# A mixture-of-experts tail on one Trainium2 core: pair table on ScalarE, another pair numbering, a shorter lead, more of the weighted sum on TensorE

## The chip, the cores and the metric

The kernel runs on one core of one Trainium2 chip. The metric is the device time of one execution in microseconds (us). A core has five engines with instruction queues of their own: TensorE (PE, with its weight loads shown apart as PEld), VectorE (DVE), ScalarE (ACT), GpSimd (POOL) and SyncE (SP), which here issues the plain DMA transfers; POOL issues the indirect ones (gathers and scatters by an index table).

## The reference

A decoder of two layers works on 8 sequences of 128 tokens of 256 numbers, all float32. Each layer has attention, cross-attention and a feed-forward part, with a layer normalisation after each. The change touches only the last part, a mixture of 64 experts of which each token uses 8:

```python
logits = x @ gate_w.T                       # 1024 tokens, 64 experts
probs = softmax(logits); w, idx = top_k(probs, 8)
combine = (one_hot(idx, 64) * w[..., None]).sum(axis=1)
for e in range(64):
    h = silu(x @ w13[e][:128].T) * (x @ w13[e][128:].T)
    acc += combine[:, e:e+1] * (h @ w2[e].T)
x = layernorm(x + acc)
```

## The kernel before

Up to about 676 us the kernel computes everything ahead of the experts; this part is the same in both versions, but for one small POOL operation. After that come four stages.

**The pair table (L845 to L879).** There are 1024 x 8 = 8192 pairs of a token and a chosen expert. They are sorted by expert into 64 blocks (NG) of 128 rows. For each pair its place in the sorted order is known (`blk_f`, `row_f`), and the inverse is wanted: which pair stands at each place. It is found with 0/1 matrices. For each of the 8 sequences b, DVE makes `is_blk` (L852, 8 x 64 per token) and `is_row` (L862, 8 x 128). ACT multiplies `is_blk` by the token's row number plus one into `no[:, 0]` (L857), and POOL multiplies it by the turn number b*8+k+1 into `no[:, 1]` (L858, with the row `turn_no`). Eight matmuls per sequence (`pair_in`, L868) add these up in PSUM, all sequences into one result, with the row in its one half and the turn in its other. Five DVE operations (L872 to L879) turn this into `pairs`, the row of the DRAM array `pair_rows` to which a pair's result is written, and `tok_i`, the token to gather. The pair number is (b*8 + k)*128 + s for token s of sequence b.

**The visits (`run_visits`).** A block may hold rows of several experts, so the unit of work is a visit of one expert to one block. Here 104 visits (FEW, the arm "few") are executed. Visit and block have the helpers:

- `gather(g)`, L923: POOL gathers the 128 token rows of block g by an indirect DMA into a ring of 6 buffers `xg`.
- `turn(g)`, L933 and L934: PE transposes the block, and DVE copies it from PSUM into its place in the long array `cols`.
- `fetch(v)`, L943: SP fetches the expert's weights of visit v, 384 KB, into the ring `wring` of 10 buffers.
- `hidden(v)`, L955: eight matmuls; then Silu on ACT (L963) and the product on DVE (L965). `begins` gives the column at which the visit begins, as a register.
- `down(v)`, L972: four matmuls, and ACT copies the result back into `cols` (L975) over the input.
- `turn_back(g)`, L982 to L985: PE transposes the finished block, DVE copies it, and POOL scatters its rows to `pair_rows`.
- `weight(b)` (L888 to L895) and `spread(b)` (L903) on DVE: the eight combine weights of each token of sequence b, and for each of the first ON_PE = 4 of them a 128 x 128 diagonal matrix `diag`.

The order on PE and POOL is written by hand as one loop over steps. The other engines' order is set by a scheduler. The loop's body, for steps from -8:

```python
if 0 <= step < count:            hidden(step)
if 0 <= step + LEAD < NG:        turn(step + LEAD)        # LEAD = 4
if 0 <= step - 2 < count:        down(step - 2)
if 0 <= step + 8 < count:        fetch(step + 8)
if 0 <= step + 8 < NG:           gather(step + 8)
if 0 <= step - 3 - spare < NG:   turn_back(step - 3 - spare)
if 0 <= step < 12 * B and step % 12 == 11: weight(...); spread(...)
```

`spare` is 104 - 64 = 40: block g can be written over by visits up to g + 40, so its scatter comes 43 steps after.

**The tail (L1022 to L1039).** For each sequence SP loads its 8 x 128 pair rows, 1 MB, into a tile `z` (L1027) of a pool with four buffers. PE adds up the first four of the eight weighted terms by matmuls with the diagonals (`moe_sum`, L1030, each float32 matmul being two instructions), DVE adds the other four to the residual (L1034), then the two are added (`moe_r`, L1036) and normalised (`layernorm`: L177, L179 and L182 on DVE, L171 and L172 on POOL between them). SP writes the result `y` out (L1039).

Of the kernel before, what the change touches and what calls it, by code (L numbers as in the profile page):

```python
# [9 lines left out]
F32 = mybir.dt.float32  # L10
I32 = mybir.dt.int32
BF16 = mybir.dt.bfloat16
AF = mybir.ActivationFunctionType
ALU = mybir.AluOpType
AX = mybir.AxisListType

P = 128
B = 8
# [14 lines left out]
TOP = 8  # L33
NG = B * S * TOP // P
# [20 lines left out]
def decoder_kernel(ctx: ExitStack, tc: tile.TileContext, i, out):  # L55
    nc = tc.nc
# [21 lines left out]
    def ps_mm(name):  # L78
        return ps_of["mm"].tile([P, 512], F32, tag="mm", name=name)
# [366 lines left out]
    with tc.tile_pool(name="l0f", bufs=1) as fp:  # L446
# [51 lines left out]
        with tc.tile_pool(name="l0fh", bufs=1) as hp:  # L498
            for h in range(HALVES):
# [8 lines left out]
                for bb in range(4):  # L508
                    b = 4 * h + bb
# [17 lines left out]
    zd = dp.tile([B * TOP * S, D], F32, name="pair_rows")  # L527
    rp = ctx.enter_context(tc.tile_pool(name="route", bufs=1))
# [6 lines left out]
    iota = rp.tile([P, P], F32, name="iota")  # L535
# [2 lines left out]
    nc.gpsimd.iota(starts, pattern=[[P, P]], base=0, channel_multiplier=0, allow_small_or_imprecise_dtypes=True)  # L538
    row_no = rp.tile([P, 1], F32, name="row_no")
    nc.gpsimd.iota(row_no, pattern=[[1, 1]], base=1, channel_multiplier=1, allow_small_or_imprecise_dtypes=True)  # L540
    turn_no = rp.tile([P, B * TOP], BF16, name="turn_no")
    nc.gpsimd.tensor_scalar(turn_no, iota[:, : B * TOP], 1.0, None, ALU.add)
    comb = rp.tile([P, B, NE], F32, name="combine")
    seen = rp.tile([P, B + 1, NE], F32, name="seen")
    nc.gpsimd.memset(seen[:, 0, :], 0.0)
# [21 lines left out]
    with l1w, tc.tile_pool(name="l1a", bufs=2) as ap, tc.tile_pool(name="l1v", bufs=L1_HEADS + 2) as vp:  # L567
        scale = 1.0 / math.sqrt(P)
# [216 lines left out]
    loop = ExitStack()  # L785
# [61 lines left out]
    with tc.tile_pool(name="onehot", bufs=3) as op:  # L847
        pn = ps_mm("pair_in")[:, : 2 * NG].rearrange("p (a g) -> p a g", a=2)
        for b in range(B):
            at = slice(b * TOP, (b + 1) * TOP)  # L850
            is_blk = op.tile([P, TOP, NG], BF16, tag="is_blk", name=f"is_blk_{b}")
            nc.vector.tensor_tensor(  # L852
                is_blk, iota[:, :NG].unsqueeze(1).to_broadcast([P, TOP, NG]),
                blk_f[:, at].unsqueeze(2).to_broadcast([P, TOP, NG]), ALU.is_equal,
            )
            no = op.tile([P, 2, TOP, NG], BF16, tag="no", name=f"no_{b}")
            nc.scalar.activation(no[:, 0], is_blk, AF.Copy, scale=row_no)  # L857
            nc.gpsimd.tensor_tensor(  # L858
                no[:, 1], is_blk, turn_no[:, at].unsqueeze(2).to_broadcast([P, TOP, NG]), ALU.mult
            )  # L860
            is_row = op.tile([P, TOP, P], BF16, tag="is_row", name=f"is_row_{b}")
            nc.vector.tensor_tensor(  # L862
                is_row, iota.unsqueeze(1).to_broadcast([P, TOP, P]),
                row_f[:, at].unsqueeze(2).to_broadcast([P, TOP, P]), ALU.is_equal,
            )
            for k in range(TOP):
                n = b * TOP + k
                nc.tensor.matmul(  # L868
                    pn, is_row[:, k, :], no[:, :, k, :], start=(n == 0), stop=(n == B * TOP - 1)
                )  # L870
    s_of = rp.tile([P, NG], F32, name="s_of")
    nc.vector.tensor_scalar(s_of, pn[:, 0], -1.0 - P, None, ALU.add)  # L872
    pairs = rp.tile([P, NG], I32, name="pairs")
    nc.vector.scalar_tensor_tensor(pairs, pn[:, 1], float(P), s_of, ALU.mult, ALU.add)
    tok_b = rp.tile([P, NG], I32, name="tok_b")
    nc.vector.tensor_scalar(tok_b, pairs, 10, 7, ALU.arith_shift_right, ALU.logical_shift_left)
    tok_i = rp.tile([P, NG], I32, name="tok_i")
    nc.vector.tensor_single_scalar(tok_i, pairs, P - 1, op=ALU.bitwise_and)
    nc.vector.tensor_tensor(tok_i, tok_i, tok_b, ALU.bitwise_or)  # L879


    cw = rp.tile([P, B, TOP], F32, name="pair_weight")
    wring = loop.enter_context(tc.tile_pool(name="wring", bufs=10, side="right"))
    mp = loop.enter_context(tc.tile_pool(name="moe", bufs=3, side="right"))

    def weight(b):
# [8 lines left out]
        nc.vector.reduce_sum(cw[:, b, :], eq, axis=AX.X)  # L895


    ON_PE = 4
    diag = dgp.tile([P, B, ON_PE, P], F32, name="diag")

    def spread(b):
        for k in range(ON_PE):
            nc.vector.tensor_scalar(diag[:, b, k, :], ident, cw[:, b, k : k + 1], None, ALU.mult)  # L903

    LEAD = 4

    def run_visits(arm, count):

# [12 lines left out]
        def gather(g):  # L921
            x = mp.tile([P, D], F32, tag="xg", bufs=6, name=f"xg_{arm}_{g}")
            nc.gpsimd.indirect_dma_start(  # L923
                out=x, out_offset=None, in_=xd,
                in_offset=bass.IndirectOffsetOnAxis(ap=tok_i[:, g : g + 1], axis=0),
                bounds_check=B * S - 1, oob_is_err=False,
            )
            xg[g] = x

        def turn(g):  # L930
            pt = ps_tr(f"moe_xT_{arm}_{g}").rearrange("p (k t) -> p k t", k=4)[:, :2]
            for k in range(2):
                nc.tensor.transpose(pt[:, k, :], xg[g][:, k * P : (k + 1) * P], ident)  # L933
            nc.vector.tensor_copy(cols[:, :, (g + 1) * P : (g + 2) * P], pt)  # L934
# [14 lines left out]
        def hidden(v):  # L949
            o = begins(v, nc.tensor.engine, fed)  # L950
            ps = ps_mm(f"moe_gu_{arm}_{v}")[:, :D].rearrange("p (a t) -> p a t", a=2)
            for a in range(2):
                for k in range(2):
                    at = k * D + a * P
                    mm = nc.tensor.matmul(  # L955
                        ps[:, a, :], ws[v][:, at : at + P], cols[:, k, bass.ds(o + P, P)],
                        start=(k == 0), stop=(k == 1),
                    )

                    tc.declare_no_dep(mm.ins, group=f"left_{arm}", reason="columns of earlier visits")  # L960
            fed.append(mm.ins)
            s = mp.tile([P, P], F32, tag="s", name=f"moe_s_{arm}_{v}")
            nc.scalar.activation(s, ps[:, 0, :], AF.Silu)  # L963
            hid = mp.tile([P, P], F32, tag="hid", bufs=4, name=f"moe_h_{arm}_{v}")
            nc.vector.tensor_tensor(hid, ps[:, 1, :], s, ALU.mult)  # L965
            hs[v] = hid

        def down(v):
            ps = ps_o(f"moe_o_{arm}_{v}")[:, :D].rearrange("p (c t) -> p c t", c=2)
            for c in range(2):  # L970
                at = 2 * D + c * P
                nc.tensor.matmul(ps[:, c, :], ws[v][:, at : at + P], hs[v], start=True, stop=True)  # L972
            o = begins(v, nc.scalar.engine, left)

            cp = nc.scalar.copy(cols[:, :, bass.ds(o, P)], ps)  # L975
            left.append(cp.ins)
            tc.add_to_no_dep_group(f"left_{arm}", cp.ins)
# [17 lines left out]
        with tc.manual_schedule(engines={nc.tensor.engine, nc.gpsimd.engine}):  # L995
            for step in range(-8, count + 4):
                if 0 <= step < count:
                    hidden(step)
                if 0 <= step + LEAD < NG:
                    turn(step + LEAD)  # L1000
                if 0 <= step - 2 < count:
                    down(step - 2)
                if 0 <= step + 8 < count:
                    fetch(step + 8)
                if 0 <= step + 8 < NG:
                    gather(step + 8)
                if 0 <= step - 3 - spare < NG:
                    turn_back(step - 3 - spare)
                if 0 <= step < 12 * B and step % 12 == 11:
                    weight(step // 12)  # L1010
                    spread(step // 12)
# [5 lines left out]
    with tc.If(few == NE) as enough:  # L1017
        run_visits("few", FEW)
    with enough.Else():
        run_visits("all", NV)  # L1020

    loop.close()  # L1022
    tp = ctx.enter_context(tc.tile_pool(name="tail", bufs=4, side="right"))
    zv = zd.rearrange("(b k s) d -> b s k d", b=B, k=TOP)
    for b in range(B):
        z = tp.tile([P, TOP, D], F32, tag="z", name=f"z_{b}")
        nc.sync.dma_start(out=z, in_=zv[b])  # L1027
        ps = ps_mm(f"moe_sum_{b}")[:, :D]
        for k in range(ON_PE):
            nc.tensor.matmul(ps, diag[:, b, k, :], z[:, k, :], start=(k == 0), stop=(k == ON_PE - 1))  # L1030

        acc = x5[b // 2][:, b % 2, :]
        for k in range(ON_PE, TOP):
            nc.vector.scalar_tensor_tensor(acc, z[:, k, :], cw[:, b, k : k + 1], acc, ALU.mult, ALU.add)  # L1034
# [67 lines left out]
```

## Time and profile before

| | us |
|---|---|
| median of 3 runs (lowest, highest) | 964.62 (963.94, 969.0) |
| the profiled execution | 968.18 |
| its span, from first to last instruction | 966.5 |
| pair table: first is_blk to the end of tok_i | 676.55 to 699.79 |
| first gather issued | 700.84 |
| first hidden starts | 708.83 |
| last scatter issued | 917.29 |
| first z issued, first moe_sum | 921.58, 927.60 |
| last y computed (end) | 963.23 |

Times within the profile count from the start of its span. The profile lists for each engine which work was busy when, what ended an idle time (the releaser), and which share of full speed the TensorE clock was granted (0.909 over the span). A group of instructions is named by line, engine and the tensors out<-in. A matmul's end is modelled. The DMA figures are the busy share of the core's 16 DMA engines and the rate.

### The profile page before, as it was taken

How to read it: one execution, taken by the hardware profiler on the slowest of the kernel's cores; microseconds unless marked ns; L12 is line 12 of the kernel's file. 1: busy time of each engine (PE TensorE's matmuls, PEld its weight loads, DVE VectorE, ACT ScalarE, POOL GpSimd, SP SyncE). 2: the span in 40 equal slices, each digit the busy share in tenths (PEclk: the TensorE clock that was granted, in tenths of full speed). 3: DMA queues.
4: the chain of work that ended last, by engine and by line, in shares of the span. 5: the costliest groups of instructions: out<-in, count | busy, mean ns of one | idle time of the engine just before them, and what ended most of it. 6: DMA issues, size and time to landing. Idle time of an engine off the chain costs nothing.

```text
span 966.5 us, 14470 instructions
## 1 busy us (share of the span) xinstructions
PE 825.1 (85%) x4650; PEld 557.1 (58%) x4650; DVE 484.6 (50%) x1312; ACT 280.3 (29%) x968; POOL 249.1 (26%) x333
## 2 busy tenths in 40 slices
PE   7999976699999999999989699994369986999743
PEld 3555533356655557755547455552259986988632
DVE  2899655421344442344441377765867342433346
ACT  2677411022133331133330033321213331333200
POOL 0000144201400000000000623111776665554611
PEclk9999977589999999999998799986569998999968
DMA  7800000410000000000000100000449986888475
GB/s 234 308 1 2 1 1 0 123 59 1 0 1 1 0 1 1 0 1 0 1 1 1 43 2 13 13 12 12 163 129 305 328 299 195 265 290 294 132 230 169
DMA packets 46259, 87.66 MB, mean 91 GB/s; under 512 B 6112, under 2 KB 23872, under 8 KB 46176
## 3 DMA queue, kind: packets, MB, share of 16 engines
q1 hardware_dynamic: 40032, 69.85, 22.5%
q0 software_dynamic: 6144, 16.79, 5.1%
q8 instruction: 42, 0.69, 0.3%
q14 instruction: 41, 0.34, 0.1%
HBM read 76.13 MB, written 10.49 MB: 90 GB/s over the span
## 4 chain that ended last, share of the span: by engine, by line
PE 64%; DVE 15%; POOL 7%; issue 5%; DMA 4%; ACT 2%; another core or an unknown queue 1%; SPq 1%; POOLq 0%; ACTq 0%; DVEq 0%
PE moe_gu_few L955 8%; PE l_y L609 6%; PE l_v L577 6%; PE l_q L577 6%; PE l_k L577 6%; PE moe_o_few L972 4%; PE l_c L600 3%; PE l_s L592 3%; PE down L514 3%; PE y_s L662 3%; PE up L504 2%; DVE maxima L668 2%; DVE l_e L220 2%; ACT l_e L213 2%; PE moe_xT_few L933 2%
## 5 line engine op out<-in xcount | busy, mean ns | idle before, releaser
L213 ACT ACTIVATE l_e<-l_s,nm_l 128x128 f32<-128x128 f32 x256 | 90.2, 368 | 109.2 <-DVE nm_l L210 108.9
L955 PE MATMUL moe_gu_few<-cols,w_few 128*128 (+1 forms) x832 | 116.6, 285 | 1.5 <-issue 0.6
L955 PEld LDWEIGHTS moe_gu_few<-cols,w_few 128*128 128x128 f32 x832 | 106.1, 200 | 5.6 <-issue 5.2
L985 POOL DMA_INDIRECT pair_rows<-moe_os_few,pairs x64 | 63.4, 991 | 54.7 <-DVE moe_os_few L984 35.9
L923 POOL DMA_INDIRECT xg_few<-x_rows,tok_i x64 | 66.3, 1036 | 36.2 <-issue 14.0
L171 POOL TENSOR_SCALAR rs_l1a<-mv_l1a 128x1 f32<-128x1 f32 x8 | 1.8, 221 | 269.2 <-DVE mv_l1a L179 269.2
L972 PE MATMUL moe_o_few<-moe_h_few,w_few 128*128 128x128 f32 x416 | 65.9, 282 | 0.0
L691 ACT ACTIVATE y_e<-y_sT 128x512 f32<-128x512 f32 x64 | 33.0, 604 | 94.5 <-PE y_sT L684 94.5
L577 PE MATMUL l_q<-xT_l1a,w_qkv 128*128 128x512 f32 x128 | 60.2, 593 | 0.0
L577 PE MATMUL l_v<-xT_l1a,w_qkv 128*128 128x512 f32 x128 | 60.1, 592 | 0.0
L577 PE MATMUL l_k<-xT_l1a,w_qkv 128*128 128x512 f32 x128 | 60.1, 592 | 0.0
L609 PE MATMUL l_y<-w_o,l_vs 128*128 128x256 f32 x256 | 57.3, 387 | 0.0
L972 PEld LDWEIGHTS moe_o_few<-moe_h_few,w_few 128*128 128x128 f32 x416 | 57.0, 199 | 0.1
L220 DVE TENSOR_SCALAR l_e<-l_e,inv_l 128x128 f32<-128x128 f32 x256 | 55.7, 282 | 1.4
L963 ACT ACTIVATE moe_s_few<-moe_gu_few 128x128 f32<-128x128 f32 x104 | 28.9, 279 | 92.4 <-PE moe_gu_few L955 39.5
L609 PEld LDWEIGHTS l_y<-w_o,l_vs 128*128 128x128 f32 x256 | 50.0, 196 | 8.5 <-issue 1.5
L934 DVE COPY cols<-moe_xT_few 128x256 f32<-128x256 f32 x64 | 26.9, 421 | 52.6 <-PE moe_gu_few L955 17.9
L213 ACT ACTIVATION_READ_ACCUMULATOR l_e<-l_s,nm_l 128x1 f32 x256 | 52.9, 206 | 0.0
L601 DVE TENSOR_TENSOR l_vs<-l_c,l_vs 128x512 f32<-128x512 f32 x32 | 22.1, 692 | 60.5 <-PE l_c L600 60.5
L975 ACT COPY cols<-moe_o_few 128x256 f32 (+1 forms) x104 | 38.8, 373 | 44.4 <-PE moe_o_few L972 11.6
L965 DVE TENSOR_TENSOR moe_h_few<-moe_gu_few,moe_s_few 128x128 f32<-128x128 f32 x104 | 29.7, 287 | 41.5 <-ACT moe_s_few L963 25.8
L210 DVE TENSOR_REDUCE nm_l<-l_s 128x4 f32<-128x512 f32 x64 | 43.3, 686 | 10.6 <-PE l_s L592 8.6
(258 smaller groups left out, 1430.6 us busy)
## 6 DMA issues: line engine op xcount, KB each, us to landing
w_few<-in_experts SPq DMA_DIRECT2D x104, 384.0 KB
z<-pair_rows SPq DMA_DIRECT2D x8, 1024.0 KB
w_qkv<-in_w_qkv SPq DMA_DIRECT2D x8, 768.0 KB
w_o<-in_w_o SPq DMA_DIRECT2D x1, 2048.0 KB
xT<-in_xT SPq DMA_DIRECT2D x2, 512.0 KB
x<-in_x SPq DMA_DIRECT2D x4, 256.0 KB
cx<-in_ctx SPq DMA_DIRECT2D x1, 1024.0 KB
q_up<-in_up_qT SPq DMA_DIRECT2D x4, 256.0 KB
```

Of the source, the lines that this page charges most:

```text
L210: nc.vector.tensor_reduce(nm, s, AX.X, ALU.max, negate=True)
L213: nc.scalar.activation(e[:, a, :], s[:, a, :], AF.Exp, bias=nm[:, a : a + 1], scale=1.0, accum_out=sums[:, a : a + 1],)
L220: nc.vector.tensor_scalar(e[:, a, :], e[:, a, :], inv[:, a : a + 1], None, ALU.mult)
L577: nc.tensor.matmul(ps, w_qkv[:, k, c, n, :], xT[h][:, k, :], start=(k == 0), stop=(k == 1))
L609: nc.tensor.matmul(py[:, :D], scaled[h, m][:, bb * S : (bb + 1) * S], w_o[:, m, :], start=(m == 0), stop=(m == L1_HEADS - 1),)
L691: nc.scalar.activation(e, tiles[j], AF.Exp)
L923: nc.gpsimd.indirect_dma_start(out=x, out_offset=None, in_=xd, in_offset=bass.IndirectOffsetOnAxis(ap=tok_i[:, g : g + 1], axis=0), bounds ...
L955: mm = nc.tensor.matmul(ps[:, a, :], ws[v][:, at : at + P], cols[:, k, bass.ds(o + P, P)], start=(k == 0), stop=(k == 1),)
L965: nc.vector.tensor_tensor(hid, ps[:, 1, :], s, ALU.mult)
L972: nc.tensor.matmul(ps[:, c, :], ws[v][:, at : at + P], hs[v], start=True, stop=True)
L975: cp = nc.scalar.copy(cols[:, :, bass.ds(o, P)], ps)
L985: inst = nc.gpsimd.indirect_dma_start(out=zd, out_offset=bass.IndirectOffsetOnAxis(ap=pairs[:, g : g + 1], axis=0), in_=o, in_offset=None, ...
```

## The change

Six edits, all in the last part of the kernel:

1. `no[:, 1]` is made by ACT, in eight activations of 128 x 64 with the turn number as an immediate scale, instead of one POOL operation of 128 x 512. `no[:, 0]` is multiplied by eight times the row number (`row_8`, which takes the place of `turn_no`).
2. The pair number is now token*8 + k, with the token b*128 + s. Six DVE operations make `pairs` and `tok_i` instead of five.
3. `LEAD` is 2 instead of 4, and the gather is issued 6 steps ahead instead of 8. The ring `xg` still has 6 buffers.
4. `ON_PE` is 6 instead of 4: 48 diagonals instead of 32, six terms on PE and two on DVE per sequence.
5. `wring` has 9 buffers instead of 10.
6. The tail's pool has 8 buffers instead of 4. With the new numbering the 8 pair rows of one token lie together, so that z is read in pieces of 8 KB per partition instead of eight of 1 KB.

The order on PE and POOL stays as the loop gives it. SP's order in the tail is z0, z1, z2, z3, out0, z4, out1, z5, out2, out3, z6, out4, z7 and the rest of out; before it was z0 to z3, out0, out1, z4, out2, z5, out3, z6, out4, z7.

```diff
-    turn_no = rp.tile([P, B * TOP], BF16, name="turn_no")
-    nc.gpsimd.tensor_scalar(turn_no, iota[:, : B * TOP], 1.0, None, ALU.add)
+    row_8 = rp.tile([P, 1], F32, name="row_8")
+    nc.gpsimd.tensor_scalar(row_8, row_no, 8.0, None, ALU.mult)
...
-            nc.scalar.activation(no[:, 0], is_blk, AF.Copy, scale=row_no)
-            nc.gpsimd.tensor_tensor(
-                no[:, 1], is_blk, turn_no[:, at].unsqueeze(2).to_broadcast([P, TOP, NG]), ALU.mult
-            )
+            nc.scalar.activation(no[:, 0], is_blk, AF.Copy, scale=row_8)
+            for k in range(TOP):
+                nc.scalar.activation(no[:, 1, k], is_blk[:, k], AF.Copy, scale=float(b * TOP + k + 1))
...
-    s_of = rp.tile([P, NG], F32, name="s_of")
-    nc.vector.tensor_scalar(s_of, pn[:, 0], -1.0 - P, None, ALU.add)
+    n_of = rp.tile([P, NG], I32, name="n_of")
+    nc.vector.tensor_scalar(n_of, pn[:, 1], -1.0, None, ALU.add)
+    seq = rp.tile([P, NG], I32, name="seq")
+    nc.vector.tensor_scalar(seq, n_of, 3, 10, ALU.arith_shift_right, ALU.logical_shift_left)
+    nc.vector.tensor_single_scalar(n_of, n_of, TOP - 1, op=ALU.bitwise_and)
+    nc.vector.tensor_tensor(n_of, n_of, seq, ALU.bitwise_or)
     pairs = rp.tile([P, NG], I32, name="pairs")
-    nc.vector.scalar_tensor_tensor(pairs, pn[:, 1], float(P), s_of, ALU.mult, ALU.add)
-    tok_b = rp.tile([P, NG], I32, name="tok_b")
-    nc.vector.tensor_scalar(tok_b, pairs, 10, 7, ALU.arith_shift_right, ALU.logical_shift_left)
+    nc.vector.scalar_tensor_tensor(pairs, pn[:, 0], -8.0, n_of, ALU.add, ALU.add)
     tok_i = rp.tile([P, NG], I32, name="tok_i")
-    nc.vector.tensor_single_scalar(tok_i, pairs, P - 1, op=ALU.bitwise_and)
-    nc.vector.tensor_tensor(tok_i, tok_i, tok_b, ALU.bitwise_or)
+    nc.vector.tensor_single_scalar(tok_i, pairs, 3, op=ALU.arith_shift_right)
...
-    wring = loop.enter_context(tc.tile_pool(name="wring", bufs=10, side="right"))
+    wring = loop.enter_context(tc.tile_pool(name="wring", bufs=9, side="right"))
...
-    ON_PE = 4
+    ON_PE = 6
...
-    LEAD = 4
+    LEAD = 2
...
-                if 0 <= step + 8 < NG:
-                    gather(step + 8)
+                if 0 <= step + 6 < NG:
+                    gather(step + 6)
...
-    tp = ctx.enter_context(tc.tile_pool(name="tail", bufs=4, side="right"))
-    zv = zd.rearrange("(b k s) d -> b s k d", b=B, k=TOP)
+    tp = ctx.enter_context(tc.tile_pool(name="tail", bufs=B, side="right"))
+    zv = zd.rearrange("(b s k) d -> b s k d", b=B, k=TOP)
```

## The prediction

> **What bounds the kernel now.** The profiled execution took 968.18 us: a span of 966.5 and 1.68 around it. The median of the runs shown is 964.62, so I work on the profiled time and subtract 3.6 at the end. About 0.5% (4.8 us) is what a measurement of this kernel can tell from no change. Nothing before the pair table at 676 us is touched but one small POOL operation, so I read first the busy time by stage (window, length, then busy us and instructions of PE, PEld, DVE, ACT, POOL, then granted clock, DMA share, GB/s):
>
> ```profile
> 680.00:700.00 20.00, 8.07 (x64) 6.65 (x63) 16.75 (x18) 4.33 (x6) 14.84 (x8) 0.50 0.49 185
> 700.00:720.00 20.00, 10.75 (x66) 9.46 (x67) 11.54 (x30) 2.84 (x7) 14.08 (x13) 0.67 0.30 82
> 720.00:760.00 40.00, 40.00 (x334) 39.78 (x333) 27.58 (x85) 14.47 (x46) 24.99 (x24) 0.93 0.93 310
> 760.00:800.00 40.00, 35.98 (x310) 34.50 (x309) 15.02 (x47) 13.14 (x43) 25.08 (x25) 1.00 0.90 306
> 800.00:840.00 40.00, 32.83 (x237) 30.78 (x238) 15.06 (x44) 9.97 (x32) 22.78 (x24) 0.87 0.73 218
> ...
> 940.00:966.00 26.00, 9.32 (x32) 6.58 (x32) 16.22 (x40) 0.00 (x0) 4.82 (x12) 0.84 0.59 186
> ```
>
> The limits differ by stage: DVE and POOL in the table (680 to 700), PE in the visits after 720, with the DMA close behind; in the tail no engine is full. The waits name them (engine, line, releaser: us in total, times, longest):
>
> ```profile
> PE moe_sum L1030 <- DMA z<-pair_rows: 23.1, 5, 13.1
> ...
> PE pair_in L868 <- POOL no L858: 14.3, 7, 6.6
> ...
> PE moe_xT_few L933 <- DVE cols L934: 10.8, 4, 3.2
> ```
>
> The timeline of the table's last two sequences shows the period (start, duration, engine, operation):
>
> ```profile
> 678.42 0.67 DVE L852 TENSOR_TENSOR is_blk<-iota,blk_f 128x512 bf16<-128x512 f32 x1
> ...
> 693.14 1.89 POOL L858 TENSOR_TENSOR no<-is_blk,turn_no 128x512 bf16<-128x512 bf16 x1 [0.69 <-DVE is_blk L852]
> 694.05 1.52 DVE L852 TENSOR_TENSOR is_blk<-iota,blk_f 128x512 bf16<-128x512 f32 x1
> ...
> 695.67 0.72 ACT L857 ACTIVATE no<-is_blk,row_no 128x512 bf16<-128x512 bf16 x1 [1.86 <-DVE is_blk L852]
> 695.72 1.89 POOL L858 TENSOR_TENSOR no<-is_blk,turn_no 128x512 bf16<-128x512 bf16 x1 [0.69 <-DVE is_blk L852]
> ```
>
> POOL's product starts every 2.58 us (693.14, 695.72), and is_blk takes 1.52 beside it, 0.67 when alone. And the tail's last sequences:
>
> ```profile
> 953.70 0.41 DVE L182 TENSOR_SCALAR y<-moe_r,mv_l1f,rs_l1f 128x256 f32<-128x256 f32 x1 [0.98 <-POOL rs_l1f L172]
> 954.03 2.04 DVE L1034 SCALAR_TENSOR_TENSOR x<-z,pair_weight,x 128x256 f32<-128x256 f32 x4
> ...
> 955.90 1.97 PE L1030 MATMUL moe_sum<-z,diag 128*128 128x256 f32 x8 [2.08 <-DMA z<-pair_rows]
> 956.17 0.42 DVE L1036 TENSOR_TENSOR moe_r<-moe_sum,x 128x256 f32<-128x256 f32 x1
> ```
>
> DVE goes round in 4.57 us (y at 953.70, the next at 958.27), 2.04 of it for four weighted additions; PE sums a sequence in 1.97 and waits for z.
>
> [...]two Silus of 0.28 start 0.20 apart (712.27 and 712.47). [...]before reads z in 1 KB rows only, so no line here shows what 8 KB gives. [...]moe_sum took 3.42 for eight instructions after 5.04 of idling (943.57), 1.97 otherwise.
>
> **The change part by part.**
>
> *Table.* POOL's eight L858 go. [...]DVE without POOL beside it needs 1.73 (is_blk at 678.42, the next at 680.15). [...]1.0 for the last eight matmuls gives 692.7, against 697.66 + 1.01 = 698.7 before. That is **-6.0**; the pair arithmetic has six DVE operations for five (+0.2): **-5.8**. PE, the gathers and all visits stand behind it. Bounds: [...]at DVE's pace -6.5. Nothing else stands in ACT's queue there (4.33 us busy of 20). The first weights, ten of 384 KB issued from 677.84 on, take 13 us at the 300 GB/s of the visits and land by 691, so the earlier hidden 0 doesn't wait for them.
>
> *Head of the visits.* With LEAD 2 only blocks 0 and 1 are turned ahead of hidden 0, which came at 708.83 behind turns at 704.45, 705.54, 707.03 and 708.38. It can start some 2.3 us earlier. Against it: 16 more DVE diagonals, at 0.20 to 0.28 each (+3.2 to +4.5), sit among the cols copies and h products, and DVE was full at 719 to 740 (20.83 of 21). So a copy of cols is late, and PE waits for it. I take **+1**, from -3 to +4. POOL's first gathers come every 1.3 us as before; gather 6 ahead and turn 2 ahead keep the distance of four steps, each gather being the same DMA on POOL's queue.
>
> *Steady visits, 14 matmul pairs in 1.56 us.* Turn to hidden falls from four steps to two: 3.1 us, less hidden and turn themselves, leaves about 2.1 for a copy whose result came 0.8 to 1.5 after the turn. **0**, hidden by that slack; the cost without it is in the rivals. The ring of 9 weights instead of 10 makes each fetch wait one down longer (1.56): weights landed some 6.2 ahead of use, 4.7 are left. **0**; SP's fetches stay in order and only their wait grows. Without that cover, PE runs at the DMA's pace, 93% busy already.
>
> *Scatters.* They begin at step 43 in either kernel; POOL then issues a gather and a scatter each step, 2 x (1.02 + 0.31) = 2.66 us, and a step takes 2.87, against 1.86 later on. Before, gathers 51 to 63 fall there, now 49 to 63: two more such steps, 2 x 1.0 = **+2** (0 if POOL catches up later, +4 if PE's clock drops). Token order changes the destination rows, not their number or size: 0, between -2 and +2, since no row shows it.
>
> *Tail.* DVE loses two of four additions, 2 x 0.50 = 1.0 per sequence; PE gains four instructions, 12 x 0.246 = 2.95. z arrives in 8 KB pieces, with eight buffers. But SP's order is z0 to z3, out0, z4, out1, z5, out2, out3, z6, out4, z7: z4 still stands behind y0, and z6 behind y3, so the eight buffers are not all used. First z at 927.6 as before (the last scatter and its landing stay), y0 near 934.6, z4 issued there instead of 937.96 and in use 5.6 later; y4 near 946, z7 issued there instead of 950.01, landed by 952.5; 2.95 of matmuls and 2.9 from r to y end y7 near 958.3, against 963.23: **-5**. Bounds: -8 with z in 3 us instead of 5.6; +2 if PE falls to half clock (12 x 0.428 = 5.1 a sequence). After the additions the late thing is z again.
>
> The sum: -5.8 + 1 + 0 + 2 - 5 = **-7.8**: 960.4 profiled, 956.8 on the scale of the median; I say 956.5.
>
> **The rivals.**
> 1. *Likeliest:* table and tail both shorten, the visits keep PE's pace: 951 to 960. Chance 0.55.
> 2. *Part of it is lost:* short activations do not overlap (table 0), or z behind y makes the tail's gain nothing. -7.8 + 5.8 = -2, or -7.8 + 5 = -2.8: 962 to 963. For it: ACT has one queue, and SP's order is unchanged at its head. Against it: the Silus' 0.20. Chance 0.20.
> 3. *More is gained:* hidden 0 earlier with no DVE delay, z at its bandwidth: -6.5 - 3 - 8 + 1 = -16.5, about 948. For it: 8 KB pieces; against it: DVE full at the head. Chance 0.11.
> 4. *Slower: cols becomes the wait.* With two steps of slack the copy L934 stands in DVE's queue behind diagonals, weights (three operations of 0.69) and h products. One weight with its six diagonals is 2.1 + 1.3 = 3.4 us, more than the slack of 2.1, so PE stops; idling may then halve its clock. It ends above +4.8 when the visits lose more than 12.6 us, 0.20 for each of the 62 turned in the loop. At 0.4 each, 25 us: 968.18 + 17 profiled, 982 by the median. For it: the four waits of PE for cols shown above, 10.8 us even with LEAD 4. Against it: after 760 DVE is busy 15 of 40. A weaker form, 0.25 each, gives 968. Chance 0.14.
>
> That the change does not do what it says: the eight z buffers are that case, and counted.
>
> **How the numbers follow.** Cases 1 and 3 are faster by over 0.5% (under 959.8): 0.66. Case 2 lies within: 0.20. Case 4 is slower (over 969.4): 0.14. The range takes case 1 whole, case 2, the inner half of case 3 and the weak end of case 4: 947 to 968.
>
> **What would show it.** Right: no L858, pair_in's waits on ACT, the first gather near 695 instead of 700.84; [...]visits 6 to 43 at 1.56; L1034 twice per sequence, the last y some 5 us closer to the last scatter. Wrong: [...]PE waits for cols of over 10 us in total; hidden waiting for w; the period of 2.87 extending over more than 15 steps; moe_sum at 5.1 each.

## The result, and the profile after

| | before | after |
|---|---|---|
| median of 17 runs (lowest, highest) | 965.32 us (957.52, 970.83) | 957.57 us (955.31, 962.2) |
| the profiled execution | 968.18 | 956.69 |
| its span | 966.5 | 955.0 |

The ratio is 0.9918, 95% interval 0.9899 to 0.9938: 7.8 us faster, where 7.8 was worked out and 956.5 stated. That the two agree to a tenth is luck, as the last part of the account shows. The profiled executions differ by more, 11.5, because that of before lay 2.9 above its median and that of after 0.9 below.

The busy time by stage in the profile after (columns as before: window, length, busy us of PE, PEld, DVE, ACT, POOL, clock, DMA share, GB/s):

```profile
680.00:700.00 20.00, 9.70 (x66) 6.41 (x66) 16.72 (x29) 13.11 (x67) 3.53 (x3) 0.50 0.56 190
700.00:720.00 20.00, 15.32 (x113) 13.96 (x113) 15.51 (x46) 5.44 (x15) 13.85 (x14) 0.93 0.56 178
720.00:760.00 40.00, 39.12 (x339) 38.01 (x338) 25.46 (x83) 14.87 (x47) 23.48 (x23) 1.00 0.91 305
...
920.00:955.00 35.00, 23.91 (x96) 19.21 (x96) 17.94 (x48) 0.00 (x0) 6.55 (x16) 0.89 0.63 240
```

In the table POOL is gone (14.84 to 3.53, and those are three gathers that start earlier), ACT has its work (13.11). PE is busy 39.12 of 40 at 720 to 760, where it was 40.00 before. In the tail it works 23.91 of 35. Its waits, one of them new:

```profile
PE moe_sum L1030 <- DMA z<-pair_rows: 13.3, 3, 12.0
...
PE pair_in L867 <- ACT no L859: 4.1, 4, 2.2
...
PE moe_gu_few L955 <- DVE cols L934: 2.6, 3, 1.8
PE moe_xT_few L933 <- DVE cols L934: 2.6, 1, 2.6
```

The third line has no counterpart in the profile before: `hidden` itself waits for `cols`. The timeline of the table after:

```profile
690.29 0.67 DVE L852 TENSOR_TENSOR is_blk<-iota,blk_f 128x512 bf16<-128x512 f32 x1
...
691.25 0.70 ACT L857 ACTIVATE no<-is_blk,row 128x512 bf16<-128x512 bf16 x1
691.86 1.25 ACT L859 ACTIVATE no<-is_blk 128x64 bf16<-128x64 bf16 x8
692.15 1.28 PE L867 MATMUL pair_in<-no,is_row 128*128 128x128 bf16 x8 [0.50 <-DVE is_row L861]
```

Eight small activations take 1.25 together, and is_blk is back at 0.67. And lines of the tail's last loads:

```profile
937.39 0.42 DVE L182 TENSOR_SCALAR y<-moe_r,mv_l1f,rs_l1f 128x256 f32<-128x256 f32 x1 [0.98 <-POOL rs_l1f L172]
...
938.22 0.42 SPq L1027 DMA_DIRECT2D z<-pair_rows  x1
...
940.77 0.42 SPq L1027 DMA_DIRECT2D z<-pair_rows  x1
...
943.41 5.70 PE L1030 MATMUL moe_sum<-z,diag 128*128 128x256 f32 x24 [3.05 <-DVE y L182]
```

z6 is issued at 938.22, behind the result y3 (937.39), and z7 at 940.77, behind y4 (939.95), although eight buffers are there. PE idles 3.05 before the last two sequences. The profile puts this wait down to a DVE result, but it ends 5.19 after the issue of z6, about the time that a load takes here (4.93 for the first), so what PE waited for was z6. For z7 it does not wait: the last two sums run on without a break.

By stage, the time of each of the two profiled pairs (the second on one of the chips of the experiments, where before takes 944 us; stages are cut at instruction starts in the traces, the last y at its end):

| stage | before | after | diff. | before, other chip | after, other chip | diff. |
|---|---|---|---|---|---|---|
| start to first is_blk | 676.55 | 677.99 | +1.4 | 680.4 | 683.1 | +2.8 |
| table: first is_blk to first gather | 24.29 | 17.88 | -6.4 | 24.29 | 17.88 | -6.4 |
| first gather to hidden 0 | 8.00 | 5.24 | -2.8 | 7.86 | 5.31 | -2.6 |
| hidden 0 to 18 | 34.95 | 36.49 | +1.5 | 30.51 | 32.88 | +2.4 |
| hidden 18 to 43 | 38.96 | 38.96 | 0 | 38.96 | 38.96 | 0 |
| hidden 43 to 64 | 55.78 | 57.40 | +1.6 | 44.99 | 46.55 | +1.6 |
| hidden 64 to last scatter | 78.77 | 77.67 | -1.1 | 67.66 | 67.38 | -0.3 |
| last scatter to last y | 45.95 | 40.31 | -5.6 | 46.31 | 40.59 | -5.7 |

### The profile page after: what moved, and what is told of

It reads as the page before. It is cut to its first block, busy times and chain, and to the rows that moved or that the text cites. A ratio compares the mean times of both kernels' runs of the same rounds, so it can differ in the third digit from the quotient of the medians.

```text
span 955.0 us, 14609 instructions
## 1 busy us (share of the span) xinstructions
PE 830.0 (87%) x4682; PEld 558.7 (59%) x4682; DVE 476.2 (50%) x1313; ACT 289.3 (30%) x1032; POOL 231.6 (24%) x325
## 5 line engine op out<-in xcount | busy, mean ns | idle before, releaser
L955 PEld LDWEIGHTS moe_gu_few<-cols,w_few 128*128 128x128 f32 x832 | 104.0, 196 | 14.8 <-issue 8.1
```

The source lines that it names most:

```text
L955: mm = nc.tensor.matmul(ps[:, a, :], ws[v][:, at : at + P], cols[:, k, bass.ds(o + P, P)], start=(k == 0), stop=(k == 1),)
```

## The experiments

All are changes of the kernel after, unless they say otherwise. They ran on three chips of the same kind, where before had a median of 944 to 945 us; each ratio is to runs of before on the same chip. The reference is the kernel after itself.

**The kernel before and the kernel after, again.**

> The kernel before, unchanged, profiled on the chips of the experiments, where its median is 944 to 945 us instead of 965. Theory: the whole difference lies in the visits (the three waits of some 4.5 us for a queue that the profile doesn't name, and slower steps from visit 43 on), the table (24.3 us) and the tail (last scatter to last y, 45.9) being the same. Then stage times of these runs can be set beside the first two profiles for table and tail, and only against each other for the visits.

946.22 in its one run; the stages are in the table above. Table and tail agree with the first profile within 0.4 us. The visits are shorter, above all from 43 on (44.99 for 55.78, 67.66 for 78.77), and the first 18 too (30.51 for 34.95). As expected. PE's four waits for `cols`, 10.8 us, which the prediction counted for rival 4, are not in this profile at all: they belong to the first chip's longer visits.

> The changed kernel, unchanged, on the chips of the experiments: the reference of all the runs that undo one edit. If the change is worth as much here as on the first chip, 0.992 of before, 937 us; table 17.9, visits 0 to 18 in 32.9 (10.5 and 22.4, as in the runs that left the head alone), last scatter to last y 40 to 41.

Median 937.44, ratio 0.9925 (0.9909 to 0.9942). The change is worth as much here as on the first chip.

**The table on POOL again.**

```diff
+    turn_no = rp.tile([P, B * TOP], BF16, name="turn_no")
+    nc.gpsimd.tensor_scalar(turn_no, iota[:, : B * TOP], 1.0, None, ALU.add)
...
-            for k in range(TOP):
-                nc.scalar.activation(no[:, 1, k], is_blk[:, k], AF.Copy, scale=float(b * TOP + k + 1))
+            nc.gpsimd.tensor_tensor(
+                no[:, 1], is_blk, turn_no[:, at].unsqueeze(2).to_broadcast([P, TOP, NG]), ALU.mult
+            )
```

> The changed kernel, but no[:,1] is made by POOL again, in one 128x512 product beside the one activation on ACT (with the new numbering). If the table is worth what the two traces say, first is_blk to first gather goes from 17.9 back to about 24.3 us and the time rises by 6.4, to about 964. Rival: POOL's product costs less than that because the table is only one of several things that the first gather and the first weights wait for; then the rise is under 3 us.

Median 945.32, ratio 1.0009 (0.9992 to 1.0026): with this one edit undone nothing is left of the gain. First is_blk to first gather took 24.65 us. The timeline of this run has the old rows back:

```profile
693.30 1.52 DVE L854 TENSOR_TENSOR is_blk<-iota,blk_f 128x512 bf16<-128x512 f32 x1
...
694.97 1.89 POOL L860 TENSOR_TENSOR no<-is_blk,turn_no 128x512 bf16<-128x512 bf16 x1 [0.69 <-DVE is_blk L854]
```

0.0084 of 944 is 7.9 us, with about 2.3 either way, against 6.8 by the stage. The rival (under 3) falls. The other five edits, tail included, then come to nothing together, within that uncertainty. This run's own profile says the same: from the first is_blk to the last y it takes 260.2, against 260.6 in the kernel before on the other chip. The tail is 4.8 shorter there, but visits 43 to 64 take 4.4 more (49.43), with PE waiting 9.1 for gathered rows where the kernel before waited 6.9; why so long in this execution stays open. (It was a short one, 940.83, only by its start: the table begins at 675.8.)

**The lead.**

```diff
-    LEAD = 2
+    LEAD = 4
...
-                if 0 <= step + 6 < NG:
-                    gather(step + 6)
+                if 0 <= step + 8 < NG:
+                    gather(step + 8)
```

> The changed kernel with LEAD 4 and the gather 8 steps ahead. Theory: the first hidden comes 2.8 us later, but visits 2 to 18 no longer wait for cols (36.5 us for the first 18 visits go back to about 35), and the scatters meet 13 gathers instead of 15 (visits 43 to 64 from 57.4 back to about 55.8): the edit was worth about nothing, 957 to 958. Rival 1, the shorter lead is a gain: 960 to 961. Rival 2, it is a loss by cols: 953 to 954.

Median 937.8, ratio 0.9922 (0.9895 to 0.9949), the same as after. In its profile hidden 0 came 2.6 later after the first gather (7.95), hidden 0 to 18 took 31.94 (-0.9), hidden 43 to 64 took 45.31 (-1.2). So the shorter lead gave 2.6 and took 2.1: nothing that a run can tell, as the theory said. Its last scatter to last y took 43.48, though nothing in the tail was changed. In the six profiles that have the tail of the kernel after unchanged, this stage lies between 38.8 and 43.5, and differences of 2 or 3 us between single profiles of the tail are to be read against that.

**Four terms on PE.**

```diff
-    ON_PE = 6
+    ON_PE = 4
```

> The changed kernel with four terms on PE and four on DVE: 16 diagonals fewer in the first visits, two additions more per sequence in the tail. Theory: the head wins 1.5 to 3 us (visits 0 to 18 in 33.5 to 35 instead of 36.5), the tail loses 8 x 0.5 to 8 x 1.0 less what z's arrival hides: 2 to 4. Net 956 to 960. Rival, the tail is paced by z alone: the tail is unchanged and the time falls to 955.

Median 937.56, ratio 0.9939 (0.9917 to 0.996): not told from after. By stage, hidden 0 to 18 took 31.44 (-1.4) and last scatter to last y 42.67 (+2.1). The head repeats closely (32.85 to 32.92 in the six profiles on these chips that leave the lead, the diagonals and the weights alone), so 1.4 is what the 16 diagonals cost there. The tail's +2.1 lies within the spread named above, and with four terms SP's order also goes back to that of before, so what the two additions alone save in the tail is not shown.

**z in pieces of 1 KB.** The old `pairs` and `tok_i` and the old view of `pair_rows` come back:

```diff
-    zv = zd.rearrange("(b s k) d -> b s k d", b=B, k=TOP)
+    zv = zd.rearrange("(b k s) d -> b s k d", b=B, k=TOP)
```

> The changed kernel with the pairs numbered (b*8+k)*128+s again, so that z is read in pieces of 1 KB. Theory: each z takes about 1.1 us longer to arrive (6.0 instead of 4.9 from issue to the first matmul), which counts once at the start of the tail and again for z4, z6 and z7 that are issued late: 2 to 4 us more, 960 to 962; the visits are unchanged. Rival: the pieces cost nothing but at the start, 958.5; or the scatters go faster or slower with one or the other numbering, which visits 43 to 103 would show.

Median 939.17, ratio 0.9943 (0.9921 to 0.9964), 0.0018 above after: 1.7 us, within the noise. The profile shows the mechanism. From the first z to the first matmul, with 1 KB and, from the kernel after on these chips, with 8 KB:

```profile
892.69 6.20 SPq L1026 DMA_DIRECT2D z<-pair_rows  x4
898.79 13.13 PE L1029 MATMUL moe_sum<-z,diag 128*128 128x256 f32 x48 [11.94 <-DMA z<-pair_rows]
```

```profile
895.67 1.96 SPq L1027 DMA_DIRECT2D z<-pair_rows  x4
900.67 12.03 PE L1030 MATMUL moe_sum<-z,diag 128*128 128x256 f32 x48 [10.96 <-DMA z<-pair_rows]
```

6.10 us against 5.00, and SP needs 6.20 instead of 1.96 to issue four loads (the fourth alone 3.90). Last scatter to last y grows by only 1.3 (41.93 for 40.59), which would fit the first rival, but these two profiles are not alike: in that of the kernel after the sum of the seventh sequence took 4.22 instead of 2.83. Set beside the first profile after, where it ran in 2.83 too, the time from the first z to the last y grows by 2.5 (38.5 for 36.0), and z4 takes 6.35 from its issue to its sum instead of 5.26. So the cost does come again for a late load, as the theory said; the medians cannot tell 2 us from none. The visits from 43 on took 114.7 against 113.9, so the scatters are indifferent to the numbering.

**The gather 8 steps ahead with LEAD 2.**

> The changed kernel with the gather 8 steps ahead again, LEAD 2 kept, still 6 buffers for the gathered blocks. Two gathers fewer stand among the scatters (51 to 63 instead of 49 to 63). Theory: visits 43 to 64 take 1 to 2 us less than 57.4, and the time is about 956. Rival: POOL, which now waits for each turn ahead of the gather that takes over its buffer, comes late, or the two gathers cost nothing: 957.5 or more.

Median 934.32, ratio 0.9909 (0.9878 to 0.9939), not told from after. Hidden 43 to 64 took 46.02 (-0.5), hidden 64 to last scatter 68.64 (+1.3). The last gather is issued 5.1 earlier after hidden 43 (33.43 for 38.57), and PE's waits for gathered rows in visits 43 to 64, 7.6 us in the kernel after, are gone; instead it waits 3.2 there for DVE's copies of finished blocks. The stage is hardly shorter for it, so an earlier gather alone is not what it needs.

**Four buffers for z.**

```diff
-    tp = ctx.enter_context(tc.tile_pool(name="tail", bufs=B, side="right"))
+    tp = ctx.enter_context(tc.tile_pool(name="tail", bufs=4, side="right"))
```

> The changed kernel with four buffers for z instead of eight. SP's order puts z4 behind y0 and z6 behind y3 in either case, so the theory is that four more buffers were worth little: z4 would be issued when the last reader of z0 is done (matmuls at 923.7 in the profile after, y0 at 928.2), no later than now. No change, 957 to 958.5. Rival: z5 to z7 come later by a sequence, 2 to 3 us, 960.

Median 937.28, ratio 0.9934 (0.9915 to 0.9952): no change, as expected. In its profile the tail is 3.2 longer (43.83), but not by the buffers: SP's order is the same, and z4 is issued 0.90 behind the start of y0 against 0.82. The difference lies in a later first z (4.78 after the last scatter instead of 3.59) and in slower sums (5.35 for the seventh). In SP's order the four added buffers are hardly used.

**All loads of z first.** (`issue_after` puts an operation behind the named one in the order of issue.)

```diff
+    zs, loads = [], []
     for b in range(B):
         z = tp.tile([P, TOP, D], F32, tag="z", name=f"z_{b}")
-        nc.sync.dma_start(out=z, in_=zv[b])
+        with tc.issue_after(loads[-1]) if loads else nullcontext():
+            dma = nc.sync.dma_start(out=z, in_=zv[b])
+        loads.append(dma.ins)
+        zs.append(z)
+    for b in range(B):
+        z = zs[b]
```

> The changed kernel with all eight loads of z issued one after another ahead of everything else in the tail, so that none stands behind a result on SP's queue. Theory: z4 to z7 arrive at 3 us distance, the PE or DVE sets the pace (2.95 or about 3.3 us per sequence), and last scatter to last y falls from 40.3 to about 36.5: 953 to 954. Rival: the DMA is the pace already (8 MB at some 350 GB/s is 24 us, plus 9 at the start), and only 1 us is won.

Median 929.4, ratio 0.9849 (0.9822 to 0.9876), 7.2 us below after by the ratios. Last scatter to last y fell from 40.59 to 35.65, 4.9; the other 2.3 is no more than the two ratios' uncertainty. The timeline:

```profile
895.66 4.09 SPq L1029 DMA_DIRECT2D z<-pair_rows  x8
...
900.59 23.35 PE L1036 MATMUL moe_sum<-z,diag 128*128 128x256 f32 x96 [11.91 <-DMA z<-pair_rows]
```

All eight loads are issued in 4.09 us, and the 96 matmul instructions run without a break of note: the second sum starts 5.05 after the first, and from then on one sequence follows every 2.59. So z behind y on SP's queue was the tail's limit in the kernel after; without it PE is, and the rival (DMA) falls. Only in this order are the eight buffers used. Whether four terms on PE would be better or worse with all loads first was not tried.

**The weights late.** `weight` (three operations) and `spread` (six) are cut into one operation per visit, each issued after that visit's product h:

```diff
-            nc.vector.tensor_tensor(hid, ps[:, 1, :], s, ALU.mult)
+            hm = nc.vector.tensor_tensor(hid, ps[:, 1, :], s, ALU.mult)
+            made.append(hm.ins)
...
-                if 0 <= step < 12 * B and step % 12 == 11:
-                    weight(step // 12)
-                    spread(step // 12)
+                if 0 <= step < 12 * B and step % 12 < 9:
+                    with tc.issue_after(made[-1]):
+                        if step % 12 < 3:
+                            weight(step // 12, step % 12)
+                        else:
+                            spread(step // 12, step % 12 - 3)
```

> The changed kernel with the DVE operations of the combine weights and their diagonals held back to one per visit, behind that visit's product h, where the scheduler had put them all into the first 20 visits. The first gather to the 18th visit is where DVE was full. Theory (cols is late because of what stands ahead of it on DVE): visits 0 to 18 fall from 36.5 to about 31 us, PE's pace of 1.56 being 28; the time falls by 4 to 5, to 953. Rival: PE's cold clock and the stall of 4 us at about 707 set the head, then it falls by under 1.5.

Median 928.86, ratio 0.9869 (0.9827 to 0.9911), 5.3 us below after by the ratios, whose intervals just touch; the stage is the firmer evidence. Hidden 0 to 18 took 28.63 instead of 32.88, and 28.63 again in both runs of the next section. Hidden 6 to 18 by engine, first in the kernel after, then in this one:

```profile
716.80:739.20 22.40, 21.01 (x169) 19.53 (x170) 21.41 (x69) 7.74 (x24) 14.13 (x15) 1.00 0.91 299
```

```profile
711.10:729.80 18.70, 18.70 (x170) 18.70 (x170) 10.62 (x34) 7.80 (x24) 14.30 (x14) 1.00 0.98 346
```

The clock is 1.00 in both. DVE was busy 21.41 of 22.40; with 10.62 of 18.70 the twelve visits run at PE's pace, 1.56 each. The theory holds: work that stands ahead on DVE made the head slow. That the late thing is `cols` is read from the waits (in the kernel after on these chips PE waits 1.8 for `cols` in the head and nothing for the product h). The kernel before took 20.14 for these visits on the other chip, so by the same measure 1.4 of such delay; in it the edit was not tried. PE shows as busy 21.01 in the first line for nearly the same instructions that take 18.70 in the second, so most of this waiting does not appear as idle time of PE.

**Both.**

> The changed kernel with both edits that were faster alone: the weights' DVE operations one per visit, and all loads of z first. They lie in different stages, so the theory is that the gains add up: 4.2 us in visits 0 to 18 and 5 to 6 in the tail, 927 by the sum of the two runs, faster than either kernel by 1.8%. Rival: the late weights leave the last two sequences' diagonals to visits 84 to 93, which delays the scatters by as much, or the tail waits for them: 929 to 930.

Median 927.11, ratio 0.9816 (0.9794 to 0.9839). The stages keep both gains: hidden 0 to 18 in 28.63, last scatter to last y in 34.63. The median is the 927 that the stages' sum gave. Against the kernel after the gain is clear; by the ratios it is not told from either edit alone, whose intervals overlap with this one.

> The same with the gather 8 steps ahead (LEAD 2, 6 buffers). Alone that edit gave 46.0 us for visits 43 to 64 where the others took 47.1 to 47.8. Theory: 1 us more is won, 926. Rival: visits 64 to 103 give it back (62.3 in that run against 61.2): the same as without it within 0.1%.

Median 924.79, ratio 0.9790 (0.9768 to 0.9813), the fastest version: 2.1% below before and 1.4% below after, with an interval clear of either edit alone. Whether the gather's place adds anything is open, since the two intervals overlap. Hidden 43 to 64 took 46.92 (47.27 without), hidden 64 to last scatter 68.07 (68.82).

## Why the prediction was right

The time, the direction and most sizes held, but one step was wrong, and errors of opposite sign met: the stages from the table on gained more than was worked out, and part of that was lost ahead of the table.

- *Table, -5.8:* measured -6.4 in both pairs. ACT's eight rounds took 14.41 from the first L857 to the last L859, 1.80 each, and a small activation came every 0.146. The price of the small activations, on which the -6.0 rested, no trace of the kernel before had shown. What was too long is the 1.0 for the last eight matmuls: each follows its own small activation, and the last ended 0.32 after ACT did. From there to the first gather it took 0.27 longer than before, where 0.2 was said for the sixth DVE operation.
- *Head, +1:* the earlier start gave -2.6 to -2.8 (2.3 said), the first 18 visits took +1.5 to +2.4: -1.2 and -0.2 in all. Rival 4's mechanism, `cols` late on a full DVE, is real and was shown by the late weights; it is confined to the first 18 visits and costs a fifth of the 12.6 us that the rival needed. Of its +2.4, the lead has 0.9 (undoing it) and the diagonals 1.4. (The rival's weaker form was summed wrongly: 0.25 for each of 62 blocks is 15.5, which gives 972 by the median and not 968.)
- *Steady visits, 0:* 38.96 us for 25 visits in both kernels on both chips, so the slack of two steps and nine weight buffers was enough there. This begins at visit 18 only, not at visit 6 as the sign in the prediction has it: visits 6 to 18 took 1.87 each.
- *Scatters, +2:* +1.6 in both pairs. POOL's pace was right: on the other chips it issues a gather and a scatter every 2.65 us against 2.66 worked out, 14 times in the kernel after and 12 times before (15 and 13 were said). But the two extra rounds, 5.3 us of POOL's time, are not what the stage pays for, or only in part: with the lead and the gather undone together it went back (45.31), with the gather alone it hardly did (46.02, and 46.92 in the last run; 46.55 to 47.80 in the runs that left both, but for the 49.43 of the table's run). So the lead itself seems to have most of the 1.6; by what path stays open, and the size of +2 was met in part by luck.
- *Tail, -5:* -5.6 and -5.7. Of it 1.1 to 1.2 comes from the first z reaching its sum sooner, which the sum had left at no change. The step that late loads of z still stand behind results on SP's queue, and are the late thing, held: putting all loads first won 5 us there. The load that PE waits for longest is z6 behind y3, though, and not z7, whose issue the sum followed. In the first sum the granted clock was 0.50 before (3.75 for eight instructions) and 0.58 after (4.82 for twelve), so that the 1.97 'otherwise' and the bound of +2 overlooked it; the time to y0 was taken over from before and held this in.
- *Nothing before the table is touched but one small POOL operation:* this is the step that failed. With POOL's `turn_no` gone the scheduler ordered differently in the attention at 255 us. The timeline of before, then of after, at the first scores of layer 1:

```profile
255.66 1.88 PE L577 MATMUL l_q<-xT_l1a,w_qkv 128*128 128x512 f32 x4
...
257.38 1.88 PE L577 MATMUL l_k<-xT_l1a,w_qkv 128*128 128x512 f32 x4
...
260.75 0.55 PE L194 MATMUL pt_l1a<-ident,x 128*128 128x128 f32 x3 [1.49 <-DVE x L182]
261.13 1.88 PE L577 MATMUL l_v<-xT_l1a,w_qkv 128*128 128x512 f32 x4
```

```profile
255.69 0.23 POOL L542 TENSOR_SCALAR row<-row_no 128x1 f32<-128x1 f32 x1
255.90 1.02 PE L577 MATMUL l_k<-xT_l1a,w_qkv 128*128 128x512 f32 x2
...
259.09 0.80 PE L194 MATMUL pt_l1a<-ident,x 128*128 128x128 f32 x3 [2.18 <-DVE x L182]
259.68 1.92 PE L577 MATMUL l_k<-xT_l1a,w_qkv 128*128 128x512 f32 x2
...
261.39 2.52 PE L577 MATMUL l_v<-xT_l1a,w_qkv 128*128 128x512 f32 x4
```

(The lines of before are from the other chip.) Ahead of the table these two l_k instructions and the POOL operation are the only difference in any engine's order between the two kernels. Two of the four l_k instructions now stand behind the transposes that wait for x, PE idles 2.18 instead of 1.49, the granted clock is then 0.55 from 259.00 to 261.40 (see the last section), and l_v takes 2.52 for 1.88. From the first l_q to the first score it is 7.19 us in both profiles of before, and 9.5 to 9.6 in nine of the eleven profiles that have the new order, 7.87 in the other two. The run with POOL's product has `turn_no` and the old PE order, and took 7.63. So the edit costs 0.7 to 2.4 us in a stage that it doesn't name. That run brings back the product in the table as well; a kernel that takes only `turn_no` back was not tried.

That cost is a part of why the time from the first is_blk to the end of the span falls by 12.9 in the first pair and 11.2 in the second, while the medians say -7.8 and about -7: 2.4 of 5.1, and 0.7 of 4.2. The rest is of the size of the scatter from run to run, but is not traced to a cause: the first feed-forward matmul, before which the kernels are the same, starts between 193.2 and 198.0 in the fourteen profiles, and the unchanged tails spread over 4.7 us. The predicted sum was 3 to 5 short on the stages' gain and left out this loss; that -7.8 came out is these two meeting.

## What to carry to other kernels

Price each edit in the stage where it lies, and then look at the order of the instructions on every engine, also in stages that the edit doesn't touch: here the scheduler answered to one removed operation 420 us ahead of the edit. More buffers helped here only once the queue that fills them had nothing in front that waits. And work with no near deadline is better put where its engine is idle: here the scheduler started it as soon as it could, in front of the operation that others waited for. Last, compare single profiles only in a stage that repeats: on these chips the head did to 0.1 us, the tail not to 3.

## What the runs showed of the hardware that was not expected

In the tail of before the granted clock was 0.55 in the 3.42 us of a sum that followed 5.04 of idling (943.57). It was 0.55 also after a wait of 2.18, though not in every profile: in the new order PE idles 2.18 us at 257 to 259. The clock in the windows right after, in the kernel after and in the same kernel on the other chip:

```profile
259.00:261.40 2.40, 2.31 (x6) 1.27 (x7) 0.04 (x1) 0.59 (x1) 0.00 (x0) 0.55 0.00 0
```

```profile
262.50:266.00 3.50, 2.95 (x9) 1.53 (x10) 1.11 (x2) 0.58 (x1) 0.05 (x1) 1.00 0.00 0
```

In the first the three transposes took 0.80 us instead of 0.55, the two l_k instructions behind them 1.92 instead of 1.02, and l_v 2.52 instead of 1.88; in the second, after 2.17 of idling, all took the shorter times. That is about the whole difference between 9.57 and 7.87. What decided between the two was not shown.

The same kernel took 20 us less on other chips: in the two profiles of before 21.9 less from visit 43 to the last scatter and 4.4 less in the first 18 visits, against 3.8 more ahead of the table, while the table, the steady visits and the tail agreed within 0.4 us. In the first profile of before the chain of waits holds two like this in the stage from 43 to 64, each some 4.6 us long, and the second profile has none:

```profile
796.48 4.58 another core or an unknown queue
...
816.40 4.64 another core or an unknown queue
```

They are 9 of the 10.8 us by which that stage is longer. What they wait for stays open.
